# The first layer of a graph MLP: 544 input rows as five blocks of 128 and 96, or as four of 128 and one of 32 in row groups

## The chip, the cores and the metric

The kernel runs on one core of a Trainium2 chip. Its metric is the device time of one execution in microseconds. The times come from runs on the chip; the profile and the trace come from one profiled execution, whose own time is given with them. A TensorE matmul is shown in two parts, PE (data streaming through the array) and PEld (weights being loaded). DVE is the vector engine, ACT the scalar engine, POOL is GpSimd and SP the engine that issues most of the DMAs.

## The reference

The inputs are x of 6250 nodes by 256, the destination node of each of 100,000 edges (sorted), and 96 features for each edge. Cut to what matters:

```python
x_n = layernorm(x)                                  # no scale, no offset
s   = segment_sum(edge, dst);  mx = segment_max(edge, dst)   # nodes without edges: 0
mean = s / max(count, 1)
h   = concat([x_n, s, mx, mean, u[0]])              # 256 + 3*96 + 64
g   = relu(h @ W1 + b1) @ W2 + b2 + x_n             # W1: (608, 1024), W2: (1024, 256)
x1  = x + g
p   = top2_softmax(layernorm(x1) @ gate_w + gate_b)          # 16 experts
y   = layernorm(x1) + sum_e p_e * (relu(ln @ w1_e + b1_e) @ w2_e + b2_e)
out = x1 + layernorm(y) * gamma + beta
```

All data is fp32. The part of W1 that belongs to the one global row u is folded into the bias (`c1`), so that 544 = 256 + 3·96 rows of W1 remain for each node.

## The kernel before

**Stages.** The kernel first finds where each node's edges begin and loads the weights (to about 62 us). At L1229 a value decides whether a slow path for odd inputs is taken; it isn't. Then comes the graph stage, in 13 groups of nodes. Group 0 has 2 tiles of 125 nodes, every other group 4 tiles (500 nodes). After it come 57 expert blocks of 256 rows (`run_block`), the first 14 of which are placed around the last group, and the end, which gathers the experts' rows, normalizes and writes.

**A group.** `GRP` holds the groups' tiles, and the order of the work on each engine is fixed: a list of tasks with slot numbers (`at_slot`) is sorted, and the program issues them in that order under `tc.manual_schedule()`. A group has 12 slots. With B the first slot of group g:

- Inputs: `turn(g, k)` for k = 0, 1 (the normalized x, two blocks of 128 columns) at B-6 and B-5, and for k = 2, 3, 4 (sum, max, mean, 96 columns each) at B-3, B-2, B-1. Each makes one transpose a tile into a PSUM bank `pT` (L723), and one ACT copy (L724) puts the bank into `inT`, block k.
- `hidden(g, m)` for m = 0 to 7 at slots B to B+7: 128 of the 1024 outputs for all 500 nodes, as two matmuls with `w1x` (L733, 128 rows each) and three with `w1a` (L735, 96 rows each) into one `pH` bank. The relu on ACT (L738) moves it to `hT`.
- `output(g, i)` at B+8 to B+11: for tile i, eight matmuls with `w2s` (L744) into a `pO` bank. `residual(g, i)` (L749, DVE) adds it to `xt`, one slot later.
- The group's second layernorm, gate logits (L823 counts the ranks), top 2, ranks and the sending of rows to the experts (L849) run in the slots of the next group.

**Where the edge columns come from.** Groups 0 and 1 cut windows of edges and reduce them with mask operations (`sum_window`, `sum_window_2`, `max_window`, `mask_window`); `mean_window` (L585, ACT) makes the mean. Later groups take the sums and maxima from DRAM: `edge_stream` runs over all edges in chunks; DVE multiplies, adds and takes maxima along them (L294, L295, L297, L298; the first row of a region is copied by ACT at L290, L291), SP stores the results (L305, `rows_d`) and loads the next chunk (L172, `raw`). The steps of this stream are woven between the tasks by their estimated costs. `take_edges` and `take_carry` (POOL) gather a tile's rows into `at`, `join_edges` (L702, DVE) joins what lies across a border, and `mask_edges` (L709, L710, ACT) masks and makes the mean in `a3`.

**Searches.** For later groups, ACT counts in two steps (`find_block` L461, `find_edge` L477) where each node's edges begin; `bounds` needs two small matmuls (L491, L492), which DVE takes at L597.

**PSUM.** Eight banks: one `ps` (carry sums, L379 to L405), two `pT`, two `pH`, two `pO`, one `pG` (`pg`). The experts use `pH` and `pO` too (`pB`, `pY` in `run_block`), and `sum_window_2` uses `pO`.

**Weights.** SP loads them ahead of the branch in `loads_1`: `w1x` (1 MB) and `w1a` (1.15 MB), with the loads of nodes and edge ids ahead of and behind them.

Of the kernel before, what the change touches and what calls it, by code (L numbers as in the profile page):

```python
# [19 lines left out]
P = 125  # L20
# [21 lines left out]
def kernel(  # L42
# [29 lines left out]
    FF = 512  # L72
    FC = FF // 128
    W2O = DC * FF
    B1O = W2O + FC * D
# [10 lines left out]
    assert NA <= -(-(2 * (N - P * GRP[-2][1]) - NE * (SB - 1)) // SB)  # L86
    assert NT <= GS * NE and wpack.shape[1] == WROW and D == DC * 128 and GF <= 128 and EF <= 128
    assert N0 == 2 and GW == 2 and WE <= RR * JS and P * GRP[GW - 1][0] <= EP * JR[0] <= ER // 2 and all(i == 1 for i in IB[:GW])
# [424 lines left out]
    def index_windows(g):  # L513
        a, z = GRP[g]
        n = z - a

        def tmp(name):
            return ix.tile([P, GS * max(IB)], F32, name=name)[:, 0:n]

        end, at_f, thr = tmp("end"), tmp("f"), tmp("m")  # L520
        nc.vector.tensor_copy(end, ends[g][:, :n])
        ends[g] = end
        nc.vector.tensor_scalar(at_f, end, float(-WE), 0.0, op0=OP.add, op1=OP.max)
        nc.vector.tensor_scalar(win_i[:, a - W0:z - W0], at_f, float(EF), None, op0=OP.mult)
# [6 lines left out]
        G[g]["at"] = ld.tile([P, GS, 2 * EF], F32, name="at")  # L531
        G[g]["a3"] = wk.tile([P, GS, EF], F32, name="a3")

# [30 lines left out]
    def sum_window_2(g, i, cut):  # L564
        G[g].setdefault("pw", []).append(pOp.tile([P, D], F32, name="pO")[:, 0:EF])
        for k in range(WE):
            nc.tensor.matmul(G[g]["pw"][i], ident[:P, :P], cut[:, k, :], start=(k == 0), stop=(k == WE - 1))

    def max_window(g, i):
        w = G[g]["win"][i]  # L570
        nc.vector.tensor_tensor(w, w, G[g]["mk"][:, i, 1, :, None].to_broadcast([P, WE, EF]), op=OP.min)
        over_window(w, G[g]["at"][:, i, EF:], OP.max)

    def mask_window(g, i):
        gi = G[g]["at"][:, i, :]
        j = GRP[g][0] - W0 + i
        parts = [(gi, gi, base[0][:, j, :])]
        if "pw" in G[g]:
            parts = [(gi[:, 0:EF], G[g]["pw"][i], base[0][:, j, 0:EF]), (gi[:, EF:], gi[:, EF:], base[0][:, j, EF:])]
        for o, v, b in parts:  # L580
            nc.vector.scalar_tensor_tensor(o, v, nw[:, j:j + 1], b, op0=OP.mult, op1=OP.add)

    def mean_window(g, i):
        t = GRP[g][0] + i
        nc.scalar.activation(G[g]["a3"][:, i, :], G[g]["at"][:, i, 0:EF], AF.Copy, scale=rc_n[:, t:t + 1])  # L585

# [97 lines left out]
    def take_edges(c, g, i):  # L684
        t = GRP[g][0] + i
        if i == 0:
            G[g]["at"] = ld.tile([P, GS, 2 * EF], F32, name="at")
            G[g]["a3"] = wk.tile([P, GS, EF], F32, name="a3")
        nc.gpsimd.indirect_dma_start(out=G[g]["at"][:, i, :], out_offset=None,
                                     in_=rows_d[0:EP * sum(JR[:c + 1]), :],  # L690
                                     in_offset=IndirectOffsetOnAxis(ap=first_i[:, t:t + 1], axis=0))
# [8 lines left out]
    def join_edges(g, i):  # L700
        t, gi, cg = GRP[g][0] + i, G[g]["at"][:, i, :], G[g]["cg"][i]
        nc.vector.scalar_tensor_tensor(gi[:, 0:EF], cg[:, 0:EF], cross[:, t:t + 1], gi[:, 0:EF],  # L702
# [4 lines left out]
    def mask_edges(g, i):  # L707
        t, gi = GRP[g][0] + i, G[g]["at"][:, i, :]
        nc.scalar.activation(gi, gi, AF.Copy, scale=ne_n[:, t:t + 1])  # L709
        nc.scalar.activation(G[g]["a3"][:, i, :], gi[:, 0:EF], AF.Copy, scale=rc_n[:, t:t + 1])  # L710

    def turn(g, k):
        n = GRP[g][1] - GRP[g][0]
        if "inT" not in G[g]:
            G[g]["inT"] = wk.tile([128, DC + 3, GS * P], F32, name="inT")
        rows_k = 128 if k < DC else EF
        pT = pTp.tile([128, GS * P], F32, name="pT")
        for i in range(n):
            if k < DC:
                src = G[g]["xn"][:, i, k * 128:(k + 1) * 128]  # L720
            else:
                src = G[g]["a3"][:, i, :] if k == DC + 2 else G[g]["at"][:, i, (k - DC) * EF:(k - DC + 1) * EF]
            nc.tensor.transpose(pT[:rows_k, i * P:(i + 1) * P], src, ident[:P, :P])  # L723
        nc.scalar.copy(G[g]["inT"][:rows_k, k, :n * P], pT[:rows_k, :n * P])  # L724

    def hidden(g, m):
        n = GRP[g][1] - GRP[g][0]
        inT = G[g]["inT"]
        pH = pHp.tile([128, GS * P], F32, name="pH")
        ms = slice(m * 128, (m + 1) * 128)  # L730
        for k in range(DC + 3):
            if k < DC:
                nc.tensor.matmul(pH[:, :n * P], w1x[:, k, ms], inT[:, k, :n * P], start=(k == 0), stop=False)  # L733
            else:
                nc.tensor.matmul(pH[:, :n * P], w1a[:, k - DC, ms], inT[:EF, k, :n * P], start=False,  # L735
                                 stop=(k == DC + 2))
        h = htp.tile([128, GS * P], F32, name="hT")
# [3 lines left out]
    def output(g, i):  # L741
        pO = pOp.tile([P, D], F32, name="pO")
        for m in range(HC):
# [270 lines left out]
    def run_block(b, end):  # L1014
        xT, wt, xb = (BL[b][nm] for nm in ("xT", "wt", "xb"))
        hb = MB["bk"].tile([128, FC, SB], F32, name="hb")
        pB = [pHp.tile([128, 2, SB], F32, name="pH") for _ in range(FC // 2)]

        for half in range(2):
# [10 lines left out]
            if half == 0 and b + 1 < end:  # L1030
                turn_block(b + 1)
        pY = pOp.tile([128, 2, D], F32, name="pO")
        order = [2 * i + half for half in range(2) for i in range(FC // 2)]
# [43 lines left out]
    for g, (a, z) in enumerate(GRP):  # L1077
        B, n = SLOTS * g, z - a
        if g:
# [25 lines left out]
            for k in range(DC, DC + 3):  # L1105
                at_slot(B - 3 + k - DC + (1 if g == GW and k < DC + 2 else 0), turn, g, k)
# [122 lines left out]
    with tc.If(bad_v != 0):  # L1229

        NC = (DC + 3) * GS * P - 1
        space = chp.tile([P, RR, EF], F32, name="tmp").rearrange("p r f -> p (r f)")
# [4 lines left out]
        for lo in range(0, N, NC):  # L1237
            acc = [wk.tile([128, DC + 3, GS * P], F32, name="inT").rearrange("p k n -> p (k n)")[:EF + 1] for _ in range(2)]
            nc.vector.memset(acc[0], 0.0)
            nc.vector.memset(acc[1], -BIG)  # L1240
            with tc.For_i(0, EJ, 1) as i:
# [9 lines left out]
                with tc.For_i(0, P, 5) as j0:  # L1251
                    for j in range(5):
                        v = nc.vector.value_load(dt_[0:1, ds(j0 + j, 1)], min_val=0, max_val=NC)
                        for h, op in ((0, OP.add), (1, OP.max)):
                            nc.vector.tensor_tensor(acc[h][:, ds(v, 1)], acc[h][:, ds(v, 1)], pt[:, ds(j0 + j, 1)], op=op)
            for n0 in range(0, min(NC, N - lo), P):
                n = min(P, NC - n0, N - lo - n0)
                po = pOp.tile([P, D], F32, name="pO")
                for h in range(2):
                    nc.tensor.transpose(po[:n, h * (EF + 1):(h + 1) * (EF + 1)], acc[h][:, n0:n0 + n],  # L1260
                                        ident[:EF + 1, :EF + 1])
# [10 lines left out]
    with tc.manual_schedule():  # L1272
# [23 lines left out]
        nc.sync.dma_start(w2s, w2.rearrange("(k p) d -> p k d", p=128))  # L1296
        for k in range(DC, DC + 3):
            turn(0, k)
# [126 lines left out]
```

## Time and profile before

| | |
|---|---|
| time, median of 3 runs (lowest to highest) | 1468.74 us (1467.54 to 1469.45) |
| profiled execution: its time, its span | 1468.9 us, 1467.1 us |
| granted TensorE clock, mean | 0.911 |
| busy: PE, PEld | 1182.2 us (81%), 836.7 us (57%) |
| busy: DVE, ACT, POOL | 914.6 us (62%), 498.7 us (34%), 537.0 us (37%) |
| moved by DMA | 292.23 MB, 199 GB/s |
| hidden layer, matmuls (L733 and L735) | 198.0 us (416 instructions) and 273.0 us (624) |
| output layer, matmuls (L744) | 201.3 us (800) |
| transposed blocks copied by ACT (L724) | 35.9 us (65) |

The span runs from the first to the last instruction of the trace; the time of a run is 1.8 us more. A row of a group of instructions gives their line, engine and operation, what they write and read, the shape and the count. Times within the span are in microseconds from its start. An fp32 matmul of the program stands in the trace as two weight loads and two matmul records. "A <- B" in the list of waits says that A stood idle until B had ended. Busy shares over the whole span mix stages with different limits, so each stage is read by its own window.

### The profile page before, as it was taken

The numbers are of one execution on the slowest core, as the hardware profiler recorded it, in microseconds if no ns is written. First come the engines' busy times: TensorE is split into PE (matmuls) and PEld (weight loads), VectorE is DVE, ScalarE is ACT, GpSimd is POOL, SyncE is SP. The second block draws the span as 40 slices with busy tenths as digits, with TensorE's granted clock in tenths as the row PEclk, the third lists the DMA queues.
The fourth block names the chain that finished last, engine by engine and source line by source line (L and its number), as shares of the span: only waits on it lengthen the run. The fifth ranks groups of instructions, "written<-read, shape, count | busy, mean of one in ns | idle before, by whom it ended". The sixth has DMA issues, their size and how long they took to land. (4 is left out here: it accounts for less than half of the span.)

```text
span 1467.1 us, 16077 instructions
## 1 busy us (share of the span) xinstructions
PE 1182.2 (81%) x4667; PEld 836.7 (57%) x4667; DVE 914.6 (62%) x2322; ACT 498.7 (34%) x1124; POOL 537.0 (37%) x611
## 2 busy tenths in 40 slices
PE   2858369989777879999799999898999999999200
PEld 1743144545445445655456466787888888888100
DVE  4498578969667969888678223344445544444397
ACT  3474125442426352342424431321122222122133
POOL 4134043553455644354253422233333333333100
PEclk9988579999898989999989999999999999999655
DMA  7735767787779895977886232646777787765695
GB/s 175 156 95 157 203 183 216 205 227 191 208 186 248 223 281 158 265 212 213 250 221 194 72 109 72 204 156 223 226 262 259 236 262 234 241 225 183 122 264 151
DMA packets 173538, 292.23 MB, mean 199 GB/s; under 512 B 30835, under 2 KB 119352, under 8 KB 166142
## 3 DMA queue, kind: packets, MB, share of 16 engines
q1 hardware_dynamic: 137102, 234.35, 56.0%
q0 software_dynamic: 36224, 56.33, 13.7%
q8 instruction: 40, 0.66, 0.2%
q14 instruction: 60, 0.49, 0.1%
q10 hardware_dynamic: 112, 0.41, 0.1%
HBM read 169.70 MB, written 123.21 MB: 200 GB/s over the span
## 5 line engine op out<-in xcount | busy, mean ns | idle before, releaser
L735 PE MATMUL pH<-inT,w1a 96*128 96x500 f32 (+1 forms) x624 | 273.0, 574 | 0.0
L1042 POOL DMA_INDIRECT y_d<-yb,to_i x114 | 133.7, 1173 | 293.2 <-ACT yb L1041 271.0
L744 PE MATMUL pO<-w2s,hT 128*125 128x256 f32 x800 | 201.3, 412 | 37.5 <-DVE xt L749 28.7
L1023 PE MATMUL pH<-xT,wt 128*128 128x256 f32 x912 | 223.2, 388 | 7.8 <-ACT hb L1029 6.2
L1036 PE MATMUL pO<-wt,hb 128*128 128x256 f32 x912 | 206.7, 379 | 5.4 <-DVE hb L1027 5.4
L849 POOL DMA_INDIRECT xg_d<-xr,pos_i x100 | 130.4, 1304 | 219.3 <-DVE xr L845 154.2
L733 PE MATMUL pH<-inT,w1x 128*128 128x500 f32 (+1 forms) x416 | 198.0, 601 | 5.9 <-ACT hT L738 5.9
L744 PEld LDWEIGHTS pO<-w2s,hT 128*125 128x125 f32 x800 | 161.3, 206 | 69.3 <-DVE xt L749 32.2
L735 PEld LDWEIGHTS pH<-inT,w1a 96*128 96x128 f32 x624 | 121.8, 195 | 137.7 <-issue 135.4
L1023 PEld LDWEIGHTS pH<-xT,wt 128*128 128x128 f32 x912 | 169.5, 191 | 39.8 <-ACT hb L1029 17.1
L1036 PEld LDWEIGHTS pO<-wt,hb 128*128 128x128 f32 x912 | 173.1, 190 | 29.8 <-DVE hb L1027 6.2
L1041 ACT ACTIVATE yb<-yb,xb 128x256 f32<-128x256 f32 x114 | 51.8, 500 | 345.4 <-issue 297.5
L738 ACT ACTIVATE hT<-pH,c 128x500 f32<-128x500 f32 (+1 forms) x104 | 68.5, 659 | 226.6 <-PE pH L735 226.6
L1039 DVE TENSOR_TENSOR yb<-pO,xb 128x512 f32<-128x512 f32 x57 | 39.4, 691 | 164.4 <-PE pO L1036 164.4
L470 POOL DMA_INDIRECT gb<-in_dst_dram,blk_i x50 | 78.7, 1574 | 129.7 <-DVE blk_i L467 73.2
L733 PEld LDWEIGHTS pH<-inT,w1x 128*128 128x128 f32 x416 | 79.2, 204 | 72.6 <-issue 64.3
L297 DVE TENSOR_TENSOR rw<-rw,raw 125x768 f32<-125x768 f32 x88 | 83.7, 951 | 32.5 <-DMA raw<-in_edge_dram 32.5
L294 DVE TENSOR_TENSOR rw<-rw,keep 125x768 f32<-125x768 f32 x81 | 79.4, 981 | 29.3 <-DMA rows_d<-rw 25.5
L298 DVE TENSOR_TENSOR rw<-rw,raw 125x768 f32<-125x768 f32 x88 | 85.9, 976 | 0.0
L1003 DVE COPY xT<-pT 128x512 f32<-128x512 f32 x57 | 39.4, 691 | 72.9 <-PE pT L1001 71.9
L724 ACT COPY inT<-pT 96x500 f32<-96x500 f32 (+3 forms) x65 | 35.9, 553 | 140.2 <-PE pT L723 139.9
L295 DVE TENSOR_TENSOR rw<-rw,bar 125x768 f32<-125x768 f32 x81 | 79.6, 983 | 0.0
(298 smaller groups left out, 1495.9 us busy)
## 6 DMA issues: line engine op xcount, KB each, us to landing
wt<-in_wpack_dram SPq DMA_DIRECT2D x57, 1026.0 KB
rows_d<-rw SPq DMA_DIRECT2D x27, 1440.0 KB
rows_d<-rw SPq DMA_DIRECT2D x27, 810.0 KB
raw<-in_edge_dram SPq DMA_DIRECT2D x27, 720.0 KB
xb<-xg_d SPq DMA_DIRECT2D x57, 258.0 KB
raw<-in_edge_dram SPq DMA_DIRECT2D x27, 405.0 KB
yk<-y_d SPq DMA_DIRECT2D x20, 400.0 KB
eb<-in_eb_dram SPq DMA_DIRECT2D x57, 128.0 KB
```

What stands on the lines that cost most here:

```text
L294: nc.vector.tensor_tensor(su, prev[0], keep[c][:, :, s + j, None].to_broadcast(bcast), op=OP.mult)
L295: nc.vector.tensor_tensor(mx, prev[1], bar[c][:, :, s + j, None].to_broadcast(bcast), op=OP.min)
L297: nc.vector.tensor_tensor(su, su, x_j, op=OP.add)
L298: nc.vector.tensor_tensor(mx, mx, x_j, op=OP.max)
L470: nc.gpsimd.indirect_dma_start(out=gbs_[t], out_offset=None, in_=dst_b, in_offset=IndirectOffsetOnAxis(ap=blk_i[:, t:t + 1], axis=0))
L733: nc.tensor.matmul(pH[:, :n * P], w1x[:, k, ms], inT[:, k, :n * P], start=(k == 0), stop=False)
L735: nc.tensor.matmul(pH[:, :n * P], w1a[:, k - DC, ms], inT[:EF, k, :n * P], start=False, stop=(k == DC + 2))
L744: nc.tensor.matmul(pO, G[g]["hT"][m][:, i * P:(i + 1) * P], w2s[:, m, :], start=(m == 0), stop=(m == HC - 1))
L849: d = nc.gpsimd.indirect_dma_start(out=xg_d[:, :], out_offset=IndirectOffsetOnAxis(ap=G[g]["pos"][:, i, k:k + 1], axis=0), in_=G[g]["xr"][ ...
L1023: nc.tensor.matmul(pB[i][:, half, :], wt[:, k * FF + m * 128:k * FF + (m + 1) * 128], xT[:, k, :], start=(k == 0), stop=(k == DC - 1))
L1036: nc.tensor.matmul(pY[:, h, :], hb[:, m, h * 128:(h + 1) * 128], wt[:, W2O + m * D:W2O + (m + 1) * D], start=(m == order[0]), stop=(m == o ...
L1042: d = nc.gpsimd.indirect_dma_start(out=y_d[:, :], out_offset=IndirectOffsetOnAxis(ap=BL[b]["to"][:, h:h + 1], axis=0), in_=yb[:, h, :], in ...
```

## The change

Before, 544 rows were contracted as 128, 128, 96, 96, 96. After, they are taken as four blocks of 128 rows (`w1x`, now `KC` = 4 blocks, 2 MB) and the 32 rows that remain (`KR`).

- The tile `at` has 384 columns instead of 192: sum (96), max (96), the first 64 columns of the mean, then the last 32 columns of the mean four times over. `mean()` writes both parts in two ACT operations, instead of the one that wrote `a3`, which is gone.
- `turn` takes 128 columns each time, from `at` for k = 2, 3, 4. Block 4 thus holds the last 32 input rows on each of the four row groups of the array's partitions.
- `w1r` holds the last 32 rows of W1. Row group q holds the columns of the output blocks q and q + 4. Four DMAs load it, one for each row group.
- `hidden(g, m)` for m = 0 and 4 takes four PSUM banks and issues four matmuls with 32 rows each, one in each row group, each into its own bank. They begin the sums of the output blocks m to m + 3. Each block then adds four matmuls with 128 rows. Per group this makes 32 matmuls with 128 rows and 8 with 32, instead of 16 with 128 and 24 with 96.
- One pool `acc` of five banks takes the place of `pH` and `pO` (two each) and of one of the two `pT` banks. `sum_window_2`, `hidden`, `output` and the experts' `pB` and `pY` all take their banks from it in turn.

```diff
-    w1x = wgt.tile([128, DC, HID], F32, name="w1x")
-    w1a = wgt.tile([EF, 3, HID], F32, name="w1a")
+    w1x = wgt.tile([128, KC, HID], F32, name="w1x")
+    w1r = wgt.tile([128, HC // 4, 128], F32, name="w1r")
...
-    pTp = banks.enter_context(tc.tile_pool(name="pT", bufs=2, space=PSUM))
-    pHp = banks.enter_context(tc.tile_pool(name="pH", bufs=2, space=PSUM))
-    pOp = banks.enter_context(tc.tile_pool(name="pO", bufs=2, space=PSUM))
+    pTp = banks.enter_context(tc.tile_pool(name="pT", bufs=1, space=PSUM))
+    accp = banks.enter_context(tc.tile_pool(name="acc", bufs=5, space=PSUM))
...
+    def acc(p=128):
+        return accp.tile([128, 512], F32, name="acc")[:p]
...
+    def mean(at, rc):
+
+        n = EF - KR
+        nc.scalar.activation(at[:, 2 * EF:2 * EF + n], at[:, 0:n], AF.Copy, scale=rc)
+        nc.scalar.activation(at[:, 2 * EF + n:].rearrange("p (q f) -> p q f", q=4),
+                             at[:, None, n:EF].to_broadcast([P, 4, KR]), AF.Copy, scale=rc)
+
     def mean_window(g, i):
         t = GRP[g][0] + i
-        nc.scalar.activation(G[g]["a3"][:, i, :], G[g]["at"][:, i, 0:EF], AF.Copy, scale=rc_n[:, t:t + 1])
+        mean(G[g]["at"][:, i, :], rc_n[:, t:t + 1])
...
     def hidden(g, m):
         n = GRP[g][1] - GRP[g][0]
         inT = G[g]["inT"]
-        pH = pHp.tile([128, GS * P], F32, name="pH")
+        if m % 4 == 0:
+
+            G[g]["pH"] = [acc() for _ in range(4)]
+            for q in range(4):
+                rows_q = slice(q * KR, (q + 1) * KR)
+                nc.tensor.matmul(G[g]["pH"][q][:, :n * P], w1r[rows_q, m // 4, :], inT[rows_q, KC, :n * P],
+                                 start=True, stop=False)
+        pH = G[g]["pH"][m % 4]
         ms = slice(m * 128, (m + 1) * 128)
-        for k in range(DC + 3):
-            if k < DC:
-                nc.tensor.matmul(pH[:, :n * P], w1x[:, k, ms], inT[:, k, :n * P], start=(k == 0), stop=False)
-            else:
-                nc.tensor.matmul(pH[:, :n * P], w1a[:, k - DC, ms], inT[:EF, k, :n * P], start=False,
-                                 stop=(k == DC + 2))
+        for k in range(KC):
+            nc.tensor.matmul(pH[:, :n * P], w1x[:, k, ms], inT[:, k, :n * P], start=False, stop=(k == KC - 1))
...
     def output(g, i):
-        pO = pOp.tile([P, D], F32, name="pO")
+        pO = acc(P)[:, 0:D]
...
-        nc.sync.dma_start(w1x, w1[0:D].rearrange("(k p) h -> p k h", p=128))
-        nc.sync.dma_start(w1a, w1[D:D + 3 * EF].rearrange("(k p) h -> p k h", p=EF))
+        nc.sync.dma_start(w1x, w1[0:KC * 128].rearrange("(k p) h -> p k h", p=128))
+        for q in range(4):
+            nc.sync.dma_start(w1r[q * KR:(q + 1) * KR],
+                              w1[KC * 128:KC * 128 + KR].rearrange("k (j m n) -> k m j n", m=4, n=128)[:, q])
```

More of the change, by code (lines that the diff above doesn't have):

```diff
@@ L73 @@
     FC = FF // 128
+    KC = (D + 3 * EF) // 128
+    KR = D + 3 * EF - 128 * KC
     W2O = DC * FF
@@ L86 @@
     assert NA <= -(-(2 * (N - P * GRP[-2][1]) - NE * (SB - 1)) // SB)
-    assert NT <= GS * NE and wpack.shape[1] == WROW and D == DC * 128 and GF <= 128 and EF <= 128
+    assert KR == 32 and HC % 4 == 0 and GS * P <= 512 and NT <= GS * NE and wpack.shape[1] == WROW and D == DC * 128 and GF <= 128 and EF <= 128
     assert N0 == 2 and GW == 2 and WE <= RR * JS and P * GRP[GW - 1][0] <= EP * JR[0] <= ER // 2 and all(i == 1 for i in IB[:GW])
@@ L530, in index_windows @@
         nc.vector.tensor_scalar(mk[:, :n, 1], mk[:, :n, 1], BIG, None, op0=OP.mult)
[L531 to L532 removed]
+        G[g]["at"] = ld.tile([P, GS, 128 * (KC - DC + 1)], F32, name="at")
     def take_window(g, i, w):
@@ L564, in sum_window_2 @@
     def sum_window_2(g, i, cut):
-        G[g].setdefault("pw", []).append(pOp.tile([P, D], F32, name="pO")[:, 0:EF])
+        G[g].setdefault("pw", []).append(acc(P)[:, 0:EF])
         for k in range(WE):
@@ L571, in max_window @@
         nc.vector.tensor_tensor(w, w, G[g]["mk"][:, i, 1, :, None].to_broadcast([P, WE, EF]), op=OP.min)
-        over_window(w, G[g]["at"][:, i, EF:], OP.max)
+        over_window(w, G[g]["at"][:, i, EF:2 * EF], OP.max)
     def mask_window(g, i):
-        gi = G[g]["at"][:, i, :]
+        gi = G[g]["at"][:, i, 0:2 * EF]
         j = GRP[g][0] - W0 + i
@@ L686, in take_edges @@
         if i == 0:
-            G[g]["at"] = ld.tile([P, GS, 2 * EF], F32, name="at")
-            G[g]["a3"] = wk.tile([P, GS, EF], F32, name="a3")
-        nc.gpsimd.indirect_dma_start(out=G[g]["at"][:, i, :], out_offset=None,
+            G[g]["at"] = ld.tile([P, GS, 128 * (KC - DC + 1)], F32, name="at")
+        nc.gpsimd.indirect_dma_start(out=G[g]["at"][:, i, 0:2 * EF], out_offset=None,
                                      in_=rows_d[0:EP * sum(JR[:c + 1]), :],
@@ L700, in join_edges @@
     def join_edges(g, i):
-        t, gi, cg = GRP[g][0] + i, G[g]["at"][:, i, :], G[g]["cg"][i]
+        t, gi, cg = GRP[g][0] + i, G[g]["at"][:, i, 0:2 * EF], G[g]["cg"][i]
         nc.vector.scalar_tensor_tensor(gi[:, 0:EF], cg[:, 0:EF], cross[:, t:t + 1], gi[:, 0:EF],
@@ L707, in mask_edges @@
     def mask_edges(g, i):
-        t, gi = GRP[g][0] + i, G[g]["at"][:, i, :]
+        t, gi = GRP[g][0] + i, G[g]["at"][:, i, 0:2 * EF]
         nc.scalar.activation(gi, gi, AF.Copy, scale=ne_n[:, t:t + 1])
-        nc.scalar.activation(G[g]["a3"][:, i, :], gi[:, 0:EF], AF.Copy, scale=rc_n[:, t:t + 1])
+        mean(G[g]["at"][:, i, :], rc_n[:, t:t + 1])
     def turn(g, k):
@@ L714, in turn @@
         if "inT" not in G[g]:
-            G[g]["inT"] = wk.tile([128, DC + 3, GS * P], F32, name="inT")
-        rows_k = 128 if k < DC else EF
+            G[g]["inT"] = wk.tile([128, KC + 1, GS * P], F32, name="inT")
         pT = pTp.tile([128, GS * P], F32, name="pT")
@@ L721, in turn @@
             else:
-                src = G[g]["a3"][:, i, :] if k == DC + 2 else G[g]["at"][:, i, (k - DC) * EF:(k - DC + 1) * EF]
-            nc.tensor.transpose(pT[:rows_k, i * P:(i + 1) * P], src, ident[:P, :P])
-        nc.scalar.copy(G[g]["inT"][:rows_k, k, :n * P], pT[:rows_k, :n * P])
+                src = G[g]["at"][:, i, (k - DC) * 128:(k - DC + 1) * 128]
+            nc.tensor.transpose(pT[:, i * P:(i + 1) * P], src, ident[:P, :P])
+        nc.scalar.copy(G[g]["inT"][:, k, :n * P], pT[:, :n * P])
     def hidden(g, m):
@@ L1016, in run_block @@
         hb = MB["bk"].tile([128, FC, SB], F32, name="hb")
-        pB = [pHp.tile([128, 2, SB], F32, name="pH") for _ in range(FC // 2)]
+        pB = [acc().rearrange("p (h r) -> p h r", h=2) for _ in range(FC // 2)]
         for half in range(2):
@@ L1031, in run_block @@
                 turn_block(b + 1)
-        pY = pOp.tile([128, 2, D], F32, name="pO")
+        pY = acc().rearrange("p (h d) -> p h d", h=2)
         order = [2 * i + half for half in range(2) for i in range(FC // 2)]
@@ L1104 @@
                 at_slot(B - (4 if g == GW else 5) + i // 2, mask_edges, g, i)
-            for k in range(DC, DC + 3):
+            for k in range(DC, KC + 1):
                 at_slot(B - 3 + k - DC + (1 if g == GW and k < DC + 2 else 0), turn, g, k)
@@ L1229 @@
     with tc.If(bad_v != 0):
-        NC = (DC + 3) * GS * P - 1
+        NC = (KC + 1) * GS * P - 1
         space = chp.tile([P, RR, EF], F32, name="tmp").rearrange("p r f -> p (r f)")
@@ L1237 @@
         for lo in range(0, N, NC):
-            acc = [wk.tile([128, DC + 3, GS * P], F32, name="inT").rearrange("p k n -> p (k n)")[:EF + 1] for _ in range(2)]
-            nc.vector.memset(acc[0], 0.0)
-            nc.vector.memset(acc[1], -BIG)
+            sums = [wk.tile([128, KC + 1, GS * P], F32, name="inT").rearrange("p k n -> p (k n)")[:EF + 1] for _ in range(2)]
+            nc.vector.memset(sums[0], 0.0)
+            nc.vector.memset(sums[1], -BIG)
             with tc.For_i(0, EJ, 1) as i:
@@ L1254 @@
                         for h, op in ((0, OP.add), (1, OP.max)):
-                            nc.vector.tensor_tensor(acc[h][:, ds(v, 1)], acc[h][:, ds(v, 1)], pt[:, ds(j0 + j, 1)], op=op)
+                            nc.vector.tensor_tensor(sums[h][:, ds(v, 1)], sums[h][:, ds(v, 1)], pt[:, ds(j0 + j, 1)], op=op)
             for n0 in range(0, min(NC, N - lo), P):
                 n = min(P, NC - n0, N - lo - n0)
-                po = pOp.tile([P, D], F32, name="pO")
+                po = acc(P)[:, 0:D]
                 for h in range(2):
-                    nc.tensor.transpose(po[:n, h * (EF + 1):(h + 1) * (EF + 1)], acc[h][:, n0:n0 + n],
+                    nc.tensor.transpose(po[:n, h * (EF + 1):(h + 1) * (EF + 1)], sums[h][:, n0:n0 + n],
                                         ident[:EF + 1, :EF + 1])
@@ L1296 @@
         nc.sync.dma_start(w2s, w2.rearrange("(k p) d -> p k d", p=128))
-        for k in range(DC, DC + 3):
+        for k in range(DC, KC + 1):
             turn(0, k)
```

## The prediction

> **What bounds the kernel now.** I read the windows by stage first, then the waits of the vector engine and of TensorE in the middle stage, then single instructions in order of time. Windows over 62.7 (the first hidden layer) to 911, after which only the expert stage and the end follow. The columns are length, then busy time and count of PE, PEld, DVE, ACT and POOL, then the granted TensorE clock, the DMA share and the rate.
>
> ```profile
> core 0: us, PE busy (x) PEld busy (x) DVE busy (x) ACT busy (x) POOL busy (x), PEclk, DMA share, GB/s
> 62.70:114.10 51.40, 34.07 (x134) 27.13 (x133) 39.61 (x73) 39.29 (x130) 12.64 (x8) 0.84 0.58 129
> 114.10:219.50 105.40, 62.80 (x194) 37.20 (x194) 71.18 (x205) 31.17 (x74) 36.69 (x25) 0.75 0.67 177
> 219.50:747.80 528.30, 458.41 (x1573) 275.46 (x1572) 423.83 (x1097) 220.61 (x465) 250.79 (x230) 0.92 0.81 220
> 807.00:860.10 53.10, 53.10 (x199) 32.42 (x198) 17.65 (x75) 21.96 (x40) 22.00 (x26) 1.00 0.22 57
> 860.10:911.00 50.90, 50.90 (x179) 30.25 (x178) 8.88 (x45) 12.80 (x19) 8.27 (x13) 1.00 0.34 113
> ```
>
> TensorE fills only the last two of the thirteen groups (100% of 53.1 and of 50.9 us). In the long stretch before, it is busy 458 of 528 us at a DMA share of 0.81. Who waits for whom there (219.5 to 807; total, times, longest):
>
> ```profile
> DVE at L702 <- DMA cg<-carry_d,next_i: 34.7, 7, 12.6
> DVE rw L297 <- DMA raw<-in_edge_dram: 32.1, 9, 5.9
> DVE rw L294 <- DMA rows_d<-rw: 25.5, 8, 8.5
> ...
> DVE end L597 <- PE pg L492: 0.3, 1, 0.3
> ```
>
> ```profile
> PE pO L744 <- DVE xt L749: 22.3, 12, 3.2
> ```
>
> DVE waits for transfers (92 us) and almost never for TensorE; TensorE waits for DVE. So from 219.5 to 807 the edge sums on DVE and their transfers pace the kernel, and time that TensorE saves there turns into more waiting. One hidden layer block, from a full-clock stretch:
>
> ```profile
> 411.58 1.84 PE L733 MATMUL pH<-inT,w1x 128*128 128x500 f32 x4
> 413.26 2.68 PE L735 MATMUL pH<-inT,w1a 96*128 96x500 f32 x6
> ```
>
> Ten matmul records for five blocks (an fp32 product is two passes): the second row starts 1.68 us after four passes, so 0.42 us a pass and 0.84 a block, with 128 or with 96 rows alike; the block of outputs ends its 4.20 us when the next starts at 415.77. Last, the way into group 1, where TensorE does set the pace:
>
> ```profile
> 113.47 0.36 ACT L585 ACTIVATE a<-at,rc_n 125x96 f32<-125x96 f32 x1
> ...
> 114.12 3.55 PE L733 MATMUL pH<-inT,w1x 128*128 128x500 f32 x4
> ...
> 115.64 0.55 ACT L724 COPY inT<-pT 96x500 f32<-96x500 f32 x1
> ...
> 142.11 0.68 ACT L738 ACTIVATE hT<-pH,c 128x500 f32<-128x500 f32 x1 [2.76 <-PE pH L735]
> ...
> 142.93 0.84 ACT L290 COPY rw<-raw 125x768 f32<-125x768 f32 x1
> ...
> 144.53 9.85 SPq L305 DMA_DIRECT2D rows_d<-rw  x2
> ...
> 166.57 0.96 DVE L294 TENSOR_TENSOR rw<-raw,keep 125x768 f32<-125x768 f32 x1 [16.10 <-DMA raw<-in_edge_dram]
> ```
>
> The relu of output block 5 waits for TensorE; behind it on ACT stands the copy L290, behind that on SP's queue the store L305 and then the next load of edges, and for that load DVE waits 16.1 us. A delay of TensorE between 62.7 and 142 therefore arrives in full at 166.6, from where DVE paces.
>
> **The unknown size: four 32-row matmuls, Q.** Per group the change trades 8 x 5 blocks (33.6 us) for 8 x 4 blocks (26.88) and two quads of four 32-row products, so it saves 6.72 - 2Q. No matmul of the trace uses row groups. Bounds: the eight passes one after another cost 8 x 0.42 = 3.36 (saving nothing); wholly side by side 2 x 0.42 = 0.84 (saving 5.04). The Trainium skill, "TensorE: Matmul & The Clock Gate", Part 3 (Packing small matmuls), gives 3.07 times for four row tiles of K=32, N=512: 3.36/3.07 = 1.09. The same section says that matmuls start and end strictly in program order. With the row above (two passes for each product, on the same row group), the second pass of product q can't start before its first ends, and product q+1 comes behind it in order: its first pass runs beside q's second, its own second one pass later. That staircase is five passes, 2.1 us, saving 2.52. The rule was measured on a packing and doesn't say whether each product was one pass; I take 2.1, because the row shows two. A second rule speaks against the change: "TensorEngine Tiling (Array Packing)", Tiling Modes, says that changing the tiling mode drains TensorE. The trace has no such switch; its nearest row, a weight load of 0.19 us, would add up to 0.4 for a switch in and out, and lies between 2.1 and 3.36 anyway: it goes into the range.
>
> **Start to group 1 (slower).** (a) SP's start queue carries 4 small loads instead of 1 (w1r) and 24 DMAs instead of 21 before the branch at L1229; bytes are equal (2.2 MB). DVE waits 16.3 us for SP there. I take +0.3 (0 to 1). (b) The 32-row block is the last one turned, and is now needed first. Group 0: k=4 was copied at 62.97 to 63.33, hidden at 62.72; with two more mean instructions on ACT (0.36 each) and turns in one bank, the quad starts near 64.2 (+1.5). At half clock to about 67.7 (250-column passes of 0.43): quad 2.15, then block 0; relu 69.0 instead of 67.08, +1.9 to 2.0. DVE behind it waits for ACT twice and passes it on. (c) Group 1: the max block holds mean columns, so turn 3 waits for the mean (113.47 plus a second instruction), and turn 4 for the copy of turn 3, because the one pT bank is taken; between these copies ACT runs two block searches (L477, L461) of 0.7 to 0.8 us each. The quad starts 2.9 us later than hidden did, on top of the 2.0: 119.0. (d) There the clock is half for 3.5 us: block 0 took 5.7 us (114.12 to 119.86), now quad and block about 7.3: +1.6. Blocks 1 to 5 cost 5 x 4.2 = 21.0, now 5 x 3.36 + 2.1 = 18.9: -2.1. At the relu of block 5: 2.0 + 2.9 + 1.6 - 2.1 = +4.4. Together **+4.7** (3 to 6); for Q = 1.09 the same steps give +1.8, for 3.36 +7.3.
>
> **Middle (219.5 to 807).** Saving: nothing, the DVE waits above hide it. New wait: the first hidden block starts with the last turned block, whose copy ended 0.8 us after the hidden layer began (807.18 + 0.57 against 806.98), and the search's matmul (L491) is queued behind block 0. It comes 0.8 + Q + 3.36 - 4.20 = 2.1 us later. DVE's L597 waits for it: in groups 2, 4 and 7 DVE stood at 0, 1.1 and 1.0 us of slack, so at most 2.1 + 1.0 + 1.1 = 4.2. TensorE loses waits of 1.9 us (L744 for the residual, 22.3 in 12) through the five shared banks and often arrives earlier; I take **+2.5** (0.5 to 4.2).
>
> **End (faster).** Group 11 saves 2.52; group 12 2.52 - 0.8 for the copy = 1.7. On the way from 10 to 11 the wait for a bank goes (797.10 for the residual at 796.63), but block 0 needs the banks of three residuals, which DVE ends near 803; the old start was 806.98: 0 to -3.3, I take -1.1. **-5.3**. One bank for turns costs nothing in these groups, a whole output pass (3.6 us) lies between two turns. The expert stage (PE 371.15 of 377) keeps all its matmuls; it takes three of five banks a block, waits for none, and turns once in 7.58 us against a copy of 0.69: 0. Its cover gone, that copy would cost 57 x 0.69 = 39; nothing removes it. The wider `at` rows and the gathers into them keep their bytes: 0.
>
> Sum: 4.7 + 2.5 - 5.3 = **+1.9**: the profiled run's 1468.9 us (span 1467.1 and 1.8 around it) becomes 1470.8. That run stands 0.2 over the median of 1468.74, so **1470.6**. A measurement tells about 0.2%, 2.9 us, from nothing.
>
> **Rivals.** 1. The quad costs 1.09 or less (other side, faster). Place: the two PE-paced ends. Start +1.8, middle +0.5 (copy and quad now within DVE's slack), end -(4.54 + 3.74) and about -1.7 for the transition: -10.0. Sum -7.7: 1461. My sum is near straight in Q; it crosses zero near Q = 1.9 and 2.9 us faster near 1.6. For it: the skill's 3.07; against: the two passes. 2. Row groups do not overlap (the change doesn't do what it says): Q = 3.36, start +7.3, middle +4, end about 0: 1480. For it: nothing in the trace shows a matmul beside another. 3. TensorE paces all twelve large groups: 12 x 2.52 = 30 faster, 1438. Against it stand the DVE waits; for it only the PE share of 81%.
>
> **How the numbers follow.** Staircase 0.52, rival 1 0.23, rival 2 0.20, rival 3 0.05. The staircase's own range, from its bounds: -4 (start partly absorbed, transition -3.3) to +5: 1465 to 1474, of which a quarter is faster by over 0.2%, a half within, a quarter slower. Faster: 0.23 + 0.05 + 0.13 = 0.41; same 0.26; slower 0.20 + 0.13 = 0.33. Range for 8 in 10: it takes in most of rivals 1 and 2, 1460 to 1479.
>
> **What would show it.** In the new profile: four K=32 rows of matmul in a group whose following L-row starts 2.1 us later (1.1 or 3.4 for the rivals); hidden layer of group 1 starting at about 119; the relu of its block 5 near 146.5; the DVE load wait ending near 171; groups 11 and 12 at about 50.6 and 49.2 us with TensorE full; no gain in the window from 219.5 to 807 but more waits of PE for DVE and ACT. The prediction is wrong if the quad's spacing is not a staircase, if DVE's stretch starts no later, or if DVE's waits for transfers shrink as TensorE gets faster.

## The result

The changed kernel takes 1458.36 us (median of 6 runs, 1454.13 to 1463.87), the kernel before 1467.74 us in the runs beside it. The ratio is 0.9946, with a 95% interval from 0.992 to 0.9972. Two later sets of runs gave 0.9961 (0.9942 to 0.998) and 0.9949 (0.9927 to 0.9971). The change saves about 7 us, half a per cent. The forecast was 1470.6 us, within 1460 to 1479: too slow, and the time lies just below the range.

The term that decides is the quad of 32-row matmuls. The timeline of TensorE in the changed kernel, at the start of group 11 (columns: start, length, engine, line, what is written and read, shape, count, and in brackets the idle time before it with the releaser):

```profile
804.74 0.48 PE L731 MATMUL pT<-ident,at 125*128 125x125 f32 x3
805.89 1.12 PE L742 MATMUL acc<-inT,w1r 32*128 32x500 f32 x8 [0.67 <-ACT inT L732]
806.94 3.62 PE L747 MATMUL acc<-inT,w1x 128*128 128x500 f32 x8
```

The quad's eight passes (x8) occupy TensorE from 805.89 to 806.94, **1.05 us**. The prediction took 2.1. The starts of the single passes behind this row show how, next to those of a quad in the middle stage:

```
quad at 805.89, starts in us after it:  0.00 0.01 0.01 0.02 | 0.52 0.53 0.54 0.54
quad at 279.75, starts in us after it:  0.00 0.01 0.01 | 0.52 0.53 0.54 | 1.44 1.96
```

```profile
279.75 1.11 PE L742 MATMUL acc<-inT,w1r 32*128 32x500 f32 x6 [0.67 <-ACT inT L732]
281.19 1.10 PE L742 MATMUL acc<-inT,w1r 32*128 32x500 f32 x2 [0.32 <-DVE xt L760]
```

In the first quad the four first passes start together, and so do the four second ones. The quad at 279.75 shows why no staircase arises. Its fourth bank came late, because a residual (L760) still used it: three products ran both their passes side by side, and the fourth ran its own two later. A second pass waits for the first one of its own row group, not for the other groups.

The same three stretches of time in the changed kernel, as shown last of the kernel before (group 10 ends at nearly the same time, at 806.4 against 807.2):

```profile
core 0: us, PE busy (x) PEld busy (x) DVE busy (x) ACT busy (x) POOL busy (x), PEclk, DMA share, GB/s
...
219.50:747.80 528.30, 442.22 (x1598) 262.11 (x1597) 429.38 (x1113) 229.13 (x498) 252.71 (x235) 0.91 0.81 220
...
807.00:860.10 53.10, 52.43 (x206) 31.43 (x204) 17.72 (x75) 22.94 (x44) 27.59 (x35) 1.00 0.28 70
860.10:911.00 50.90, 49.23 (x198) 32.36 (x198) 12.95 (x53) 13.18 (x20) 10.10 (x16) 1.00 0.35 116
```

In the middle TensorE is busy 16 us less (442.22 against 458.41) of the same 528.30 us, at the same DMA share of 0.81, and yet the stage ends only 0.8 us earlier. DVE's waits from 219.5 to 807 are still those for transfers, and the wait for the search's matmul has not grown:

```profile
DVE rw L301 <- DMA raw<-in_edge_dram: 32.7, 9, 6.7
DVE at L711 <- DMA cg<-carry_d,next_i: 28.2, 7, 11.6
DVE rw L298 <- DMA rows_d<-rw: 23.7, 6, 9.2
...
DVE end L607 <- PE pg L496: 0.2, 1, 0.2
```

And the way through group 1, where TensorE sets the pace until the copy at L294 (L290 before):

```profile
115.24 0.39 ACT L590 ACTIVATE at<-at,rc_n 125x128 f32<-125x128 f32 x1
...
117.81 0.55 ACT L732 COPY inT<-pT 128x500 f32<-128x500 f32 x1
...
118.41 2.05 PE L742 MATMUL acc<-inT,w1r 32*128 32x500 f32 x8 [0.80 <-ACT inT L732]
...
144.89 0.84 ACT L294 COPY rw<-raw 125x768 f32<-125x768 f32 x1
...
146.49 9.68 SPq L309 DMA_DIRECT2D rows_d<-rw  x2
...
168.68 0.96 DVE L298 TENSOR_TENSOR rw<-raw,keep 125x768 f32<-125x768 f32 x1 [14.14 <-DMA raw<-in_edge_dram]
```

The quad starts at 118.41, where the hidden layer before started at 114.12. The copy comes 2.0 us later than before (144.89 against 142.93), and the edges that DVE waits for are there 2.1 us later (168.68 against 166.57). The start delay is real, and its sign was forecast.

### The profile page after: what moved, and what is told of

Its sections match the earlier page's. It is cut to its first block, busy times and chain, and to the rows that moved or that the text cites. A ratio compares the mean times of both kernels' runs of the same rounds, so it can differ in the third digit from the quotient of the medians.

```text
span 1460.7 us, 16116 instructions
## 1 busy us (share of the span) xinstructions
PE 1148.5 (79%) x4667; PEld 810.4 (55%) x4667; DVE 915.6 (63%) x2322; ACT 511.0 (35%) x1174; POOL 527.8 (36%) x611
## 4 chain that ended last, share of the span: by engine, by line
issue 27%; DVE 23%; DMA 18%; POOL 13%; PE 12%; ACT 3%; SPq 2%; POOLq 0%; DVEq 0%; ACTq 0%
POOL y_d L1053 9%; PE acc L747 5%; DMA raw<-in_edge_dram 5%; DMA cg<-carry_d,next_i 4%; DMA rows_d<-rw 3%; PE acc L755 3%; DVE rw L302 2%; DVE rw L299 2%; DVE rw L298 2%; DMA xg_d<-xr,pos_i 2%; DVE rw L301 2%; POOL gb L474 1%; PE acc L570 1%; DMA carry_d<-ct 1%; DVE o L1387 1%
## 5 line engine op out<-in xcount | busy, mean ns | idle before, releaser
L747 PE MATMUL acc<-inT,w1x 128*128 128x500 f32 (+1 forms) x832 | 375.9, 603 | 0.0
L747 PEld LDWEIGHTS acc<-inT,w1x 128*128 128x128 f32 x832 | 163.1, 204 | 179.1 <-issue 177.3
L1034 PE MATMUL acc<-xT,wt 128*128 128x256 f32 x912 | 225.6, 391 | 7.8 <-ACT hb L1040 6.2
L1047 PE MATMUL acc<-wt,hb 128*128 128x256 f32 x912 | 209.6, 383 | 3.6 <-DVE hb L1038 3.6
L755 PE MATMUL acc<-w2s,hT 128*125 128x256 f32 x800 | 193.5, 400 | 13.4 <-ACT hT L749 13.4
L1034 PEld LDWEIGHTS acc<-xT,wt 128*128 128x128 f32 x912 | 171.0, 193 | 40.2 <-ACT hb L1040 14.9
L1047 PEld LDWEIGHTS acc<-wt,hb 128*128 128x128 f32 x912 | 175.3, 192 | 29.0 <-DVE hb L1038 4.5
L755 PEld LDWEIGHTS acc<-w2s,hT 128*125 128x125 f32 x800 | 157.8, 201 | 39.5 <-ACT hT L749 14.2
L749 ACT ACTIVATE hT<-acc,c 128x500 f32<-128x500 f32 (+1 forms) x104 | 68.5, 658 | 209.0 <-PE acc L747 209.0
L705 POOL DMA_INDIRECT cg<-carry_d,next_i x44 | 65.1, 1481 | 36.8 <-issue 23.6
```

Of the source, the lines that this page charges most:

```text
L749: nc.scalar.activation(h[:, :n * P], pH[:, :n * P], AF.Relu, bias=c1[:, m:m + 1])
L755: nc.tensor.matmul(pO, G[g]["hT"][m][:, i * P:(i + 1) * P], w2s[:, m, :], start=(m == 0), stop=(m == HC - 1))
L1034: nc.tensor.matmul(pB[i][:, half, :], wt[:, k * FF + m * 128:k * FF + (m + 1) * 128], xT[:, k, :], start=(k == 0), stop=(k == DC - 1))
L1047: nc.tensor.matmul(pY[:, h, :], hb[:, m, h * 128:(h + 1) * 128], wt[:, W2O + m * D:W2O + (m + 1) * D], start=(m == order[0]), stop=(m == o ...
```

## The experiments

Stages of one profiled execution of each kernel, in us. Such an execution can lie some us beside the median of its kernel. "Edges" is the start of DVE's first instruction after the wait shown last; "group 10" the end of its last residual; "11 and 12" from there to the last residual of group 12; "rest" from there to the end of the span.

| kernel | edges | group 10 | 11 and 12 | rest | span |
|---|---|---|---|---|---|
| before | 166.6 | 807.2 | 104.3 | 555.6 | 1467.1 |
| before, again | 166.3 | 806.2 | 104.3 | 559.0 | 1469.6 |
| changed | 168.7 | 806.4 | 96.2 | 558.1 | 1460.7 |
| changed, again | 167.9 | 803.9 | 96.2 | 557.2 | 1457.3 |
| changed, third | 168.8 | 800.0 | 96.2 | 555.0 | 1451.2 |
| one row group | 179.9 | 827.4 | 112.6 | 555.4 | 1495.3 |
| banks only | 169.2 | 802.8 | 102.4 | 554.0 | 1459.2 |
| quad twice | 172.0 | 814.0 | 100.5 | 554.3 | 1468.8 |
| quad four times | 173.6 | 807.3 | 106.3 | 557.2 | 1470.8 |
| rest turned first | 167.7 | 802.1 | 95.4 | 554.8 | 1452.2 |
| rest turned first, again | 168.3 | 799.2 | 95.4 | 553.8 | 1448.4 |
| mean early | 168.5 | 806.3 | 95.9 | 558.1 | 1460.3 |

**The quad twice: the prediction's own value for it.**

```diff
-            for q in range(4):
+            for t in range(8):
+                q = t % 4
                 rows_q = slice(q * KR, (q + 1) * KR)
                 nc.tensor.matmul(G[g]["pH"][q][:, :n * P], w1r[rows_q, m // 4, :], inT[rows_q, KC, :n * P],
-                                 start=True, stop=False)
+                                 start=True, stop=(t < 4))
```

> Every quad is issued twice (the second one starts the sums anew), so that it costs 2.1 us, the value that the prediction took for one quad. Theory (the prediction failed by the size of the quad alone, and its sum holds for the rest): about what was predicted, 1468 to 1471 us, no faster than before by 0.2%. Rival (the middle absorbs more than the sum said, only the last two groups and the start pay): 4 x 1.05 + 3 = 7 over the changed kernel, 1464 to 1466.

Measured: 1467.59 us (14 runs), ratio to before 1.0005 (0.9986 to 1.0025). With a quad of nearly the predicted size (1.89 us instead of 2.1) the kernel can't be told from the one before. The timeline of this kernel at group 11:

```profile
814.42 1.96 PE L743 MATMUL acc<-inT,w1r 32*128 32x500 f32 x16 [0.67 <-ACT inT L732]
816.31 3.62 PE L748 MATMUL acc<-inT,w1x 128*128 128x500 f32 x8
```

The two quads take 1.89 us, so the second one adds 0.84, two passes of 0.42. Groups 11 and 12 take 100.5 us, 4.3 more than in the changed kernel and 3.8 less than before; the forecast for them was 4.2 less. The edges land at 172.0, 5.5 later than before on the mean of its two profiles; the forecast was 4.7. So within the noise the sum held, and the value put into it was wrong.

**One row group: no overlap.**

```diff
-    w1r = wgt.tile([128, HC // 4, 128], F32, name="w1r")
+    w1r = wgt.tile([KR, HC, 128], F32, name="w1r")
...
-        G[g]["at"] = ld.tile([P, GS, 128 * (KC - DC + 1)], F32, name="at")
+        G[g]["at"] = ld.tile([P, GS, 3 * EF], F32, name="at")
...
-                rows_q = slice(q * KR, (q + 1) * KR)
-                nc.tensor.matmul(G[g]["pH"][q][:, :n * P], w1r[rows_q, m // 4, :], inT[rows_q, KC, :n * P],
+                nc.tensor.matmul(G[g]["pH"][q][:, :n * P], w1r[:, m + q, :], inT[:KR, KC, :n * P],
```

The loads of `w1r` and the turn of the last block are cut to 32 rows to match.

> The four 32-row products of a quad all lie on row group 0 (one copy of the last 32 mean columns, w1r on 32 partitions); all else as in the changed kernel. Theory (the gain is the overlap of the row groups: a quad of the changed kernel takes 1.05 us): here a quad takes 8 passes of 0.42 = 3.4 us, 2.3 more. Four quads in groups 11 and 12 add 9.2, the quads ahead of the store of edge sums in groups 0 and 1 add 6 to 7, the middle 0 to 6: 1474 to 1480 us. Rival (the gain comes from the five shared banks or the 128-row blocks, not from the overlap): within 5 us of the changed kernel's 1458.

Measured: 1493.02 us, ratio 1.0185 (1.0157 to 1.0213). The direction is as the theory has it, but it is 13 us more than the theory's upper end. The timeline of this kernel at group 11:

```profile
826.59 4.67 PE L741 MATMUL acc<-inT,w1r 32*128 32x500 f32 x8 [0.65 <-issue]
831.18 5.92 PE L746 MATMUL acc<-inT,w1x 128*128 128x500 f32 x8
```

The eight passes run one after another, as expected. But they take 4.59 us, and the output block behind them lasts 5.76 us to the next line's matmul (836.94) instead of 3.46. The starts of the passes show that TensorE falls to half speed within the quad, and recovers 9.5 us after its start:

```
quad:              0.00 0.52 0.94 1.36 1.78 2.20 2.80 3.63
block behind it:   4.60 5.59 6.43 7.26 8.09 8.93 9.51 9.93
```

The granted clock over the groups 11 and 12 is below full here (window from 827.4 to 940.0):

```profile
827.40:940.00 112.60, 111.89 (x375) 64.14 (x373) 26.76 (x119) 34.96 (x62) 31.90 (x43) 0.94 0.26 80
```

In groups 2 to 12 the passes behind the first quad ran at half speed, every time; the first lengthened pass began 1.8 to 3.6 us after the quad's start. (In group 1 TensorE is at half speed when the quad starts, in all kernels.) Behind the second quad, 3.55 us between two full blocks, they never did in these groups. By the table, 7 of the 13 us stand in groups 11 and 12 (16.4 us more than in the changed kernel, where 9.2 were expected) and 5 at the edges' arrival. The clock asked for a run of its own.

**The quad four times: as long, but on all rows.** The edit is that of the quad twice, with 16 in place of 8 and `t < 12`.

> Every quad issued four times (each time the sums start anew), so eight passes or 3.5 us as in the run with one row group, but with all four row groups at work. Theory (in the run with one row group TensorE fell to half clock because 3.5 us of work on 32 rows counts as idle): no fall of the clock after the quads here, about 9.2 us for each 0.84 of a quad as in the run with the quad twice, so 1458.4 + 27 = 1485, and 6 to 9 us less than the one row group's 1493. Rival (the fall comes from the wait for the last copy and would come with any quad of this length): the passes behind the quad at 0.84 us here too, and 1493.

Measured: 1479.27 us, ratio 1.01 (1.0074 to 1.0126), 14 us less than with one row group. Timeline at group 11 and window over groups 11 and 12 (807.3 to 913.6):

```profile
806.83 3.64 PE L743 MATMUL acc<-inT,w1r 32*128 32x500 f32 x32 [0.67 <-ACT inT L732]
810.40 3.62 PE L748 MATMUL acc<-inT,w1x 128*128 128x500 f32 x8
```

```profile
807.30:913.60 106.30, 105.62 (x472) 62.83 (x464) 26.78 (x120) 35.29 (x62) 31.96 (x44) 1.00 0.28 84
```

The quads take 3.57 us, the block behind one lasts 3.46 us to the next line's matmul, as in the changed kernel, and the clock is 1.00. So equally long work, behind the same wait of 0.65 to 0.67 us, lowers the clock when only 32 rows are at work and not when all 128 are. The rival is refuted. These quads also have four times as many passes, but their number isn't what counts: the changed kernel runs blocks of 128 rows behind the same wait and a quad of 1.05 us, one pass in 0.42 us as with one row group, and its clock stays at 1.00 over groups 11 and 12. One difference is left: with one row group, the four transposes ahead of the quad also fill only 32 columns.

The expected 1485 was 6 us too high. Groups 11 and 12 grew by 10.1, four quads of 2.52, as they should, and the edges came 5.1 us later. The middle, 634 us from the edges to the end of group 10, shows no cost; but this profiled execution (1472.71 us) is the fastest of the six runs, 6.6 us under their median, so the middle can't be judged by it.

**The banks alone.** The kernel before with `pHp`, `pOp` and one bank of `pTp` replaced by the pool of five; the blocks of 128 and 96 rows stay.

```diff
+    accp = banks.enter_context(tc.tile_pool(name="acc", bufs=5, space=PSUM))
...
-        pH = pHp.tile([128, GS * P], F32, name="pH")
+        pH = bank()[:, :GS * P]
...
-        pO = pOp.tile([P, D], F32, name="pO")
+        pO = bank(P)[:, 0:D]
```

> The kernel before with the changed kernel's PSUM banks (five shared, one for turns), five blocks of 128, 128, 96, 96, 96 rows as before. Theory (the gain is matmul time): no gain from the banks, the one bank for turns delays group 1 by 1 to 3 us, and the transition from group 10 to 11 gives 1 to 3 back: 1466 to 1471 us. Rival (the banks bring the gain, since outputs no longer wait for residuals): 1458 to 1462.

Measured: 1465.24 us (14 runs), ratio 0.9993 (0.9973 to 1.0012). No gain that can be told from nothing. The wait of outputs for residuals (22.3 us in the middle before) is gone from the list of this kernel, and the largest wait of TensorE from 219 to 803 is now one that was there before too, and longer than the 27.2 us of then:

```profile
PE pT L783 <- ACT xr L774: 34.4, 20, 10.1
```

Freed of one wait, TensorE stands in the next. The one bank for turns delays the edges here as well (169.2). The 102.4 us of groups 11 and 12, against 104.3 before, come from where the stage is cut: from the first hidden matmul of group 11 to the last output matmul of group 12 it takes 103.70 us in both, and 95.87 in the changed kernel. The banks have no part in what the last two groups gain.

**Turning the 32 rows first: somewhat better than the change itself.**

```diff
-            for k in range(DC, KC + 1):
-                at_slot(B - 3 + k - DC + (1 if g == GW and k < DC + 2 else 0), turn, g, k)
+            for j, k in enumerate((KC, DC, DC + 1) if g >= GW else (DC, KC, DC + 1)):
+                at_slot(B - 3 + j + (1 if g == GW and j < 2 else 0), turn, g, k)
...
-        for k in range(DC, KC + 1):
+        for k in (KC, DC, DC + 1):
             turn(0, k)
```

> The changed kernel, but the block with the 32 remaining rows is turned ahead of the other two edge blocks (in group 1 second), so that the quad does not wait for the last copy. Theory (each hidden layer of a group begins 0.5 to 0.8 us late for that copy): groups 11 and 12 gain 0.7 each, the start 0.7 to 1.5, the middle nothing: 2 to 3 us less than the changed kernel, 1455.5. Rival (the wait is taken up elsewhere): the same as the changed kernel, 1458.

Measured: 1455.7 us (9 runs), ratio to before 0.9935 (0.9911 to 0.9958). It was run once more, together with the changed kernel:

> The kernel with the rest turned first (run before at 1455.7 us) once more, beside the changed kernel on the same chip. Theory (the quad's wait for the last copy costs 0.5 to 0.8 us a group where TensorE paces): 2 to 3 us under the changed kernel of the same call; groups 11 and 12 take 95.4 us again, 0.8 less than in the changed kernel. Rival (the first difference of 2.7 us was scatter): within 1 us of it.

> The changed kernel, for the comparison with the run beside it: 1458.4 us by both theory and rival; groups 11 and 12 take 96.2 us as in its two earlier profiles.

Measured: 1454.96 us (ratio 0.9921, 0.9894 to 0.9949), beside 1459.42 for the changed kernel. Over all its 17 runs the mean is 1455.8; the changed kernel's 28 runs have 1459.3. That is 3.5 us less, plus or minus 2.3 (twice the standard error of the two means). The timeline of this kernel at group 11 shows the wait of 0.67 us gone:

```profile
800.98 0.59 PE L731 MATMUL pT<-ident,at 125*128 125x125 f32 x4
801.50 1.12 PE L742 MATMUL acc<-inT,w1r 32*128 32x500 f32 x8
802.55 2.78 PE L747 MATMUL acc<-inT,w1x 128*128 128x500 f32 x6
```

Groups 11 and 12 take 95.4 us in both of its profiles and 96.2 in all three of the changed kernel: 0.8 of the gain, half of the 1.4 that the theory gave them. From the end of DVE's wait for SP in the start (L503) to the edges' arrival it takes 126.2 and 125.5 us, against 128.4, 128.2 and 128.5 in the changed kernel; but that wait ended later in these two profiles, so the edges came only some 0.5 us earlier. The rest of the 3.5 isn't located.

**The mean earlier in group 1.** On top of that, the last tile's mean was placed one slot earlier, and the 32 rows were turned first in group 1 too.

```diff
-                    at_slot(2 * i + 4, mean_window, g, i)
+                    at_slot(2 * i + (3 if i == n - 1 else 4), mean_window, g, i)
```

> As the kernel with the rest turned first, and in group 1 the last tile's mean is placed one slot earlier, ahead of the first edge turn, so that the block with the 32 remaining rows is turned first there too. Theory (the start delay of the changed kernel comes from the chain mean, turn, copy, quad): the relu of block 5 in group 1, 144.1 us in the changed kernel and 143.1 with the rest turned first, comes at 141 to 142; the time is 1 to 2 us under that of the rest turned first, 1454 to 1455. Rival (the searches between the copies on ACT set it, or the start is absorbed before the end): no gain over the rest turned first, 1455.7.

Measured: 1458.53 us (16 runs), ratio 0.9944 (0.9928 to 0.996). The relu of block 5 comes at 144.2 us, as in the changed kernel (143.3 to 144.3) and no earlier than with the rest turned first (143.1 and 144.1). The theory failed and the rival stands: this order gives nothing. Which of the instructions between the turns holds the start wasn't tried further.

**The kernels once more, for their scatter.**

> The changed kernel once more, beside the others on the same chip, for a direct comparison and a second profile. Theory: 1458 us; in its profile the stretch after group 12 takes about 555 us as in the other kernels, not 558, since the loss there was a fall of the clock in one execution; the middle (end of group 1 to end of group 10) between 578 and 588 us. Rival (the change makes the expert stage slower or the middle faster): again 558, and a middle clearly below that of before.

> The kernel before once more, for a second profile: how much its middle varies by itself. Theory (the 5 us by which the middle of the changed kernel was shorter are scatter of the transfers): its middle lies anywhere from 578 to 588 us, against 587.7 in the first profile. Rival (the changed kernel shortens the middle): 586 to 589 again.

Measured: 1458.39 us for the changed kernel (12 runs); the one profiled run of the kernel before took 1471.35. The theory on the rest stands in part: it is 555.6 and 559.0 in two profiles of before, 558.1, 557.2 and 555.0 in three of the changed kernel, so the 2.5 us that the first pair seemed to lose there are scatter. On the middle nothing is decided. From the end of group 1 to that of group 10 it takes 587.7 and 587.6 us before, and 582.5, 582.2 and 578.3 in the changed kernel; from the edges' arrival on it is 641 and 640 against 638, 636 and 631. It looks shorter by some 2 to 9 us. But it doesn't follow the quad's length (642 with the quad twice, 634 with the quad four times), with the banks alone it is 634 too, and the profiled executions lie beside their medians: both of before above, those of the banks alone and of the quad four times below. It is left open.

## Why the prediction was wrong

**The step that failed** is the unknown size Q: "That staircase is five passes, 2.1 us, saving 2.52." It measured 1.05 us, and the first full pass behind it takes 0.10 more than the others. The bounds were right (0.84 and 3.36). The argument between them was not: two passes for each product, and matmuls that start strictly in program order, were put together into a staircase. The trace shows the passes of different row groups starting 0.01 us apart and only passes of the same row group waiting for each other. The chance given to this case, rival 1, was 0.23. The rule of the Trainium skill that the prediction weighed ("TensorE: Matmul & The Clock Gate", Part 3, 3.07 times for four row tiles) was nearly right for fp32: 3.36 us of passes in 1.05 is 3.2, or 2.9 with the 0.10 behind it. The sentence on program order in the same section misled when it was read for the two passes of an fp32 product: at 279.75 three second passes start 0.9 us before the fourth product's first one.

**The rule on changing the tiling mode** ("TensorEngine Tiling (Array Packing)", Tiling Modes) fits a small price here. The first and the last passes of a quad take some 0.52 us instead of 0.42, and so does the first full pass after it: about 0.3 us in all, against the 0.4 allowed for. It is paid once for a run of such passes, since the second of two quads adds just 0.84. That draining is the cause isn't shown.

**The rest of the sum came out, the start in part by luck.** Rival 1 (Q = 1.09) was the case that came true. Its steps against what was measured:

| step | rival 1 said | measured |
|---|---|---|
| start, at the edges' arrival | +1.8 | +1.5 to +2.3 (three profiles against the mean of two) |
| groups 11 and 12 | -8.3 | -8.1 (all profiles) |
| the middle, with the way into group 11 | -1.2 | -9 to -2 in single profiles, not settled |
| sum | -7.7 | -6.9 to -9.4 between the medians of three sets of runs |

The path of the start held: in all twelve profiles the edges arrive 24.2 to 25.0 us after the relu of group 1's block 5 begins. That the size of the start came out right is partly luck. The loads in SP's queue were to cost 0.3 us, but DVE left its wait for SP at 40.3, 39.7 and 40.2 us instead of 41.9 and 42.8, 2.3 earlier on the mean. From there to the edges it then took 4.3 us more than before, where the steps for rival 1 come to 1.5. Whether the loads end that wait earlier is open: with the rest turned first, and the same loads, it ended at 41.5 and 42.8.

**In the middle** the saving went into waits, as forecast. TensorE's waits before and after, from 219.5 to 807:

```profile
PE pT L781 <- ACT xr L772: 27.2, 19, 9.8
PE pg L823 <- DVE mm L814: 19.8, 4, 9.1
...
PE pT L792 <- ACT xr L783: 42.3, 28, 10.5
PE pg L834 <- DVE mm L825: 28.2, 5, 11.3
```

The feared new wait of DVE for the search's matmul was 0.2 to 1.5 us in three profiles of the changed kernel; it was 1.9 with the quad twice and 3.0 with the quad four times, so it seems to grow with the quad. One sign of being wrong is not settled: DVE's three waits for transfers add up to 92 and 91 us before and to 85, 89 and 81 in the changed kernel, while waits for which the profile shows no cause rose from at most 4 to 6 to 10.

The clock, which the prediction left out here, took part too. The windows from the edges to the end of group 10, of before, of the changed kernel and of the quad four times:

```profile
166.60:807.20 640.60, 548.11 (x1887) 333.04 (x1888) 512.11 (x1325) 258.19 (x541) 296.55 (x275) 0.91 0.79 216
168.70:806.40 637.70, 522.39 (x1886) 312.87 (x1890) 513.24 (x1325) 268.28 (x581) 292.23 (x271) 0.90 0.80 217
173.60:807.30 633.70, 550.78 (x2318) 332.14 (x2322) 512.76 (x1325) 268.29 (x581) 293.66 (x271) 0.93 0.80 218
```

TensorE is busy 25.7 us less than before (24 to 31 over all profiles of the two kernels). At full clock its nine groups would save 9 x (6.72 - 2 x 1.15) = 39.8 by an estimate from the measured quad. With less work it waits more, and the clock granted is lower (0.90 against 0.91); with the long quads it is higher (0.93), and they add 28.4 us instead of 9 x 2 x 2.52 = 45.4. By this estimate the clock undoes about a third of what the change saves or adds there; why it is granted so, the traces don't show.

**Rival 2** (no overlap) is what the run with one row group built. It was priced at 1480 and measured 1493; the fall of the clock was not in the sum, and the quads of the same length that left the clock up measured 1479. **Rival 3** (TensorE paces everywhere, 30 us) is refuted by the time itself.

## What to carry to other kernels

A few rows left over from blocks of 128 are cheap if four output blocks take them at once, one in each row group: two fp32 passes for four products, plus some 0.3 us that these passes and the one behind them took longer. It pays only where TensorE sets the pace, and it helped (3.5 us, plus or minus 2.3) to turn the input first that is needed first. When a sum hangs on one unknown price, build the kernel that has the other price: issuing the step twice shows whether the sum or the price was wrong, once the trace has told what the second one adds.

## What the runs showed of the hardware

- An fp32 matmul's two passes wait for each other only within their row group. Four products of 32 rows on four row groups took 1.05 us at full clock, a second such quad right behind 0.84 more.
- Work on 32 of the 128 rows did not keep the clock up here. Behind a wait of 0.65 us, eight passes on one row group took TensorE to half speed (0.84 us a pass) from 1.8 to 3.6 us after their start on, in each of the groups 2 to 12. The same length on four row groups left it at 0.42 a pass in groups 11 and 12, and so did blocks of 128 rows. Between two full blocks, 3.55 us on one row group did no harm. The threshold isn't known. The two kernels lie 14 us apart, or 12 when each is compared with the kernel before in its own set of runs; 6.3 of it stand in groups 11 and 12.
- In the middle, where TensorE waits, the granted clock followed its load: 0.90 with less matmul work against 0.91 before, and 0.93 with the quad four times.
